# Attention with a convolved query on one core: reordering the start, shortening Newton's step, and fetching the last outputs' operands earlier

## The chip, the cores and the metric

The kernel runs on one core of one Trainium2 chip. The metric is device time in microseconds (us). A profile of one execution shows five engines: TensorE (PE, matrix products; its weight loads are listed apart as PEld), VectorE (DVE), ScalarE (ACT), GpSimd (POOL) and SyncE (SP), which issues most of the DMA transfers. Every engine works through its own instructions in order and waits on semaphores for the others.

## The reference

x has the shape 4 x 384 x 48 x 48: four images of 2304 tokens with 384 channels, in 8 heads of 48.

```python
local = lax.conv_general_dilated(x, conv_w, ...)      # depthwise, 7 x 7, then batch norm
x_norm = _layernorm(x_flat, ln_gamma, ln_beta)        # over the channels
qkv = x_norm @ qkv_w.T + qkv_b
q = q + _layernorm(local_flat, ln_gamma, ln_beta)     # the convolution joins the query
attn = softmax(einsum(q, k) * scale); out = einsum(attn, v)
out = x_flat + out @ proj_w.T + proj_b
```

All is computed in float32.

## The kernel before

**Tiles.** Channels lie on the partitions, in three chunks of 128 (in an order in which every chunk holds the 48 rows of two heads' parts at partitions 0 and 64). Tokens come in groups of 384, that is 8 image rows: 6 groups to an image (`NG`), 24 in all (`NT`). A "product" below is one matmul instruction; the profile lists each float32 product of full size as two PE records.

**Stages.** (1) The start: vectors, taps and weights are loaded and scaled, and group 0 of x is normalized. (2) A loop over the six groups of image 0: `from_x` makes values, keys and queries of group g (three value, three key, three query projections, each of three products), while the next group of x is normalized. (3) For every group t of 24, twelve slots of attention: scores, the exponential on ScalarE (`score`), and the weighted sum (`weigh`). At the beginning of images 1 to 3, `from_x` makes keys and values of that image and the output projection of the image before. (4) The tail: the output projections of the last six groups (18 projections of three products), each followed by `finish`, which adds the residual on VectorE and issues the store.

**The convolution** runs on VectorE, one instruction for a tap and a chunk (`conv_ops`), 147 to a group. For group 0 the first `PE_TAPS` = 10 taps of chunk 0 are done by TensorE instead, with diagonal matrices made on ScalarE (`make_diagonals`, `first_products`) and added by `add_products`. `convolve_first(n)` hands out n conv instructions by hand in the start and in the loop; from then on `plan` spreads them over the slots, from the count that has been done by then.

**A layer norm** (`Norm`) is: the mean over the channels by a product with `mean_w` (`mean_of`, `mean`), `centre`, `squares` on ScalarE, the mean of the squares, `root` on ScalarE (logarithm, exponential, square) and a step of Newton on VectorE (`newton`), then `scale`. For later images `few_root` and `few_newton` do the same on few numbers.

**Scale and shift of the layer norm** are folded into the weights: `scale_values` and `scale_rows` multiply them on ScalarE; `shift_rows` makes the shift's products with the weights as rows, and `columns` turns these into columns for `key_bias` and `query_bias`.

**What sets the order.** TensorE, VectorE and ScalarE have the order in which the code calls them; so have SP and POOL during the first loads. After these a scheduler orders SP's transfers. The transfers of SP and ACT share eight semaphores in turn: a transfer is issued when the one eight places before it has landed. PSUM tiles of two banks come alternately from two pools of two tiles each, `accumulator` (in the profile "o") and `ring` ("r"), through `two_banks`.

**The tail's operands.** The attention outputs of the last five groups but the very last are kept in DRAM (`hold`) and read back (`fetch`, tile "af"); `load_residual` reads x again (tile "xr"). `divide` makes the reciprocal softmax sums of a group and spreads them ("rb"). A count of sums that are out of bounds (`judge`) decides at the end whether a second, slower pass is needed, which isn't with this data.

Of the kernel before, what the change touches and what calls it, by code (L numbers as in the profile page):

```python
# [15 lines left out]
P = 128  # L16
# [13 lines left out]
AHEAD = 8  # L30
# [15 lines left out]
def unshifted_pass(  # L46
# [107 lines left out]
    nc.scalar.dma_start(out=taps_in, in_=conv_w)  # L154
    load_slab(0, 0)
    load_x(0, 0)
# [37 lines left out]
    load_x(0, 1)  # L194
    for g in range(2, NG):
        load_x(0, g)
# [64 lines left out]
    def make_diagonals():  # L261
        for i, tap in enumerate(taps[:PE_TAPS]):
            nc.scalar.mul(diagonal(i), ident, cw[:, 0, tap : tap + 1])
# [86 lines left out]
    class Norm:  # L350
# [52 lines left out]
        def root(self):  # L403

            y, u = self.buf[:, 1, :], self.buf[:, 2, :]
            nc.scalar.activation(u, self.m, AF.Ln, bias=eps)
            nc.scalar.activation(y, u, AF.Exp, scale=-0.5)
            nc.scalar.activation(u, y, AF.Square)

        def newton(self):  # L410
# [3 lines left out]
            nc.vector.scalar_tensor_tensor(u, u, -1.0, y, ALU.add, ALU.mult)  # L414
            nc.vector.scalar_tensor_tensor(y, u, -0.5, y, ALU.mult, ALU.add)
# [38 lines left out]
        def few_root(self):  # L454
# [4 lines left out]
            nc.scalar.activation(self.u, self.y, AF.Square)  # L459

        def few_newton(self):
            u, y = self.u, self.y
            nc.vector.tensor_mul(u, u, self.v)
            nc.vector.scalar_tensor_tensor(u, u, -1.0, y, ALU.add, ALU.mult)
            nc.vector.scalar_tensor_tensor(y, u, -0.5, y, ALU.mult, ALU.add)
# [3 lines left out]
        def scale(self, rs):  # L469
            nc.vector.tensor_mul(self.src, self.src, rs)  # L470
# [83 lines left out]
    row = work.tile([P, CC, P], F32, tag="rb", name="row", bufs=1)  # L554

    def of_row(i):
        return slice(0, 1) if i == 2 else slice(64, 65)

    def shift_rows(some):
        r = two_banks()  # L560
        for c in range(CC):
            for i in some:
# [6 lines left out]
                )  # L569
        for i in some:  # L570
            src, dst = r[of_row(i), i % 2, :C], row[of_row(i)]
            dst = dst.rearrange("o u (h d) -> o u h d", h=2)
            nc.scalar.copy(
                dst[:, :, :, 0:HD], src[:, 0:288].rearrange("o (u h d) -> o u h d", h=2, d=HD)
# [3 lines left out]
                src[:, 288:384].rearrange("o (h u r) -> o u h r", h=2, r=16),  # L578
            )

    def columns(some):

        m = two_banks()[:, :, 0:CC]
        for j, i in enumerate(some):
            for c in range(CC):
                nc.tensor.matmul(
                    m[:, j, c : c + 1],
                    lhsT=row[of_row(i), c, :],
# [18 lines left out]
    def key_bias(m):  # L607
        nc.vector.tensor_add(qkb[:, 1, :], qk_vec[:, 1, :], m[:, 0, :])
        nc.vector.tensor_add(vbp[:, :, 0], vbp[:, :, 0], m[:, 1, :])

    def query_bias(m):

        nc.vector.tensor_add(qkb[:, 0, :], qk_vec[:, 0, :], m[:, 0, :])
# [18 lines left out]
    def local_end(t, rs):  # L632
        acc = accs[t]
        nc.vector.tensor_mul(acc, acc, rs)
# [73 lines left out]
    def load_residual(t):  # L708
        b, g = divmod(t, NG)
        xr = work.tile([P, CC, G], F32, tag="xr", name=f"xr{t}")  # L710
# [11 lines left out]
    def fetch(t):  # L722
        ao = work.tile([P, CC, G], F32, tag="af", name=f"af{t}")
# [92 lines left out]
    make_diagonals()  # L816
    first_products(3)
    norm = Norm(xn[0, 0])
    norm.mean_of(norm.src)
    convolve_first(AHEAD)  # L820
    norm.centre()
    norm.squares()
    first_products(3)
    shift_rows((2, 1))
    scale_values()
    convolve_first(12)
    norm.mean_of(norm.buf)
    norm.root()
    first_products(4)
    m = columns((1, 2))  # L830
    for c in range(CC):
        scale_rows(1, c)
    norm.scale(norm.newton())
    key_bias(m)
    for g in range(NG):
# [4 lines left out]
        convolve_first(4)  # L840
# [5 lines left out]
        convolve_first(5)  # L846
# [3 lines left out]
        if g == 0:  # L850
            shift_rows((0,))
# [4 lines left out]
        if g == 0:  # L856
            for c in range(CC):
                scale_rows(0, c)
        next(making)
        if g == 0:  # L860
            m = columns((0,))
        convolve_first(8 if last else 13)
# [4 lines left out]
        if g == 0:  # L867
            query_bias(m)
# [5 lines left out]
    for t in range(NT):  # L874
# [52 lines left out]
        for s in range(NSLOT):  # L927
# [8 lines left out]
            if s == NSLOT - 4 and g == NG - 1:  # L936
                ao = fetch(t - g)
                if next_image:
                    for gx in range(NG - later(b + 1), NG - 1):
# [623 lines left out]
```

## Time and profile before

| what | us |
|---|---|
| median of 5 runs | 2870.2 (2867.95 to 2871.55) |
| the profiled execution's own time | 2869.94 |
| its span in the profile | 2868.2 |
| first product on TensorE | 11.48 |
| first value projection of group 0 | 29.73 |
| first scores (attention begins) | 151.17 |
| last weighted sum ends, tail begins | 2817.69 |
| last result written by VectorE | 2863.3 |

Starts and durations are in us from the start of the span. A line of the timeline gives start, duration, engine, line of the source and operation, output and inputs, the count, and in brackets how long the engine was idle before it and what released it. The time outside the span, 1.7 us in this execution, is not seen by the profile.

### The profile page before, as it was taken

Reading aid. Unit: us, or ns where it says so; the run is one execution under the profiler, and the core shown is the slowest. Engines: PE = TensorE matmul, PEld = TensorE weight load, DVE = VectorE, ACT = ScalarE, POOL = GpSimd, SP = SyncE. Lnnn points to the kernel's source line nnn. Section 1 sums busy time; section 2 is a strip of 40 time slices with the busy share of each in tenths; the row PEclk is TensorE's granted clock in tenths of the full one; section 3 lists DMA queues with packets and bytes.
Section 4 is the critical chain, followed back from the end, with each engine's and each line's share of the span. In section 5 each row is a group of like instructions: output and inputs, shape, how many; then the busy total and the mean of one; then the engine's idle time right before and its main releaser. Section 6 shows DMA issues by size and latency. Waiting matters only on the chain.

```text
span 2868.2 us, 70244 instructions
## 1 busy us (share of the span) xinstructions
PE 2835.5 (99%) x29492; PEld 1438.0 (50%) x29492; DVE 2353.2 (82%) x4661; ACT 1648.4 (57%) x2341; POOL 17.2 (1%) x82
## 2 busy tenths in 40 slices
PE   8999999999999999999999999999999999999998
PEld 4544454554554455555555445555555544444444
DVE  7999999999888888888888889888788787787302
ACT  4356666666226666666623666666642466666661
POOL 1000000000000000000000000000000000000000
PEclk9999999999999999999999999999999999999999
DMA  6101121101221111110132112102113110100004
GB/s 115 38 7 35 45 49 35 37 25 43 74 80 29 42 35 42 29 39 24 38 94 69 28 30 51 35 22 45 38 39 87 52 22 30 41 23 15 13 21 120
DMA packets 103688, 124.37 MB, mean 43 GB/s; under 512 B 43344, under 2 KB 89024, under 8 KB 103360
## 3 DMA queue, kind: packets, MB, share of 16 engines
q1 hardware_dynamic: 99568, 116.07, 16.8%
q8 instruction: 233, 3.82, 0.6%
q10 hardware_dynamic: 3088, 3.65, 0.4%
q14 instruction: 95, 0.78, 0.1%
q0 software_dynamic: 704, 0.06, 0.0%
HBM read 81.98 MB, written 27.03 MB: 38 GB/s over the span
## 4 chain that ended last, share of the span: by engine, by line
PE 95%; DVE 2%; DMA 2%; ACT 0%; issue 0%; SPq 0%; ACTq 0%; DVEq 0%
PE r L754 39%; PE o L775 39%; PE r L475 9%; PE o L475 8%; DVE acc L255 1%; DMA xn<-in_x_dram 1%; DVE xr L730 0%; DMA out_dram<-xr 0%; DMA rb<-rden 0%; DMA af<-held 0%; DMA taps_in<-in_conv_w_dram 0%; DMA staged<-in_qkv_wT_dram 0%; DMA vec<-natural 0%; DVE xn L401 0%; ACT pt L762 0%
## 5 line engine op out<-in xcount | busy, mean ns | idle before, releaser
L762 ACT ACTIVATE pt<-r 128x768 f32<-128x768 f32 x1728 | 1399.0, 810 | 757.3 <-PE r L754 741.1
L255 DVE SCALAR_TENSOR_TENSOR acc<-slab,vec,acc 128x368 f32<-128x368 f32 (+7 forms) x3447 | 1757.1, 585 | 5.5 <-DMA xn<-in_x_dram 4.4
L775 PE MATMUL o<-pt,v 64*64 64x384 f32 x13824 | 1436.6, 482 | 0.0
L754 PE MATMUL r<-xn,k 48*64 48x384 f32 x10368 | 1080.2, 482 | 3.3 <-DVE xr L730 2.0
L775 PEld LDWEIGHTS o<-pt,v 64*64 64x64 f32 x13824 | 547.7, 132 | 571.0 <-issue 547.5
L754 PEld LDWEIGHTS r<-xn,k 48*64 48x64 f32 x10368 | 412.4, 132 | 432.2 <-issue 374.3
L754 PE MATMUL r<-qt,kt 48*64 48x384 f32 x3456 | 357.7, 482 | 0.1
L754 PEld LDWEIGHTS r<-qt,kt 48*64 48x64 f32 x3456 | 133.4, 132 | 146.5 <-issue 135.9
L673 DVE TENSOR_TENSOR ao<-o,ao 113x384 f32<-113x384 f32 x72 | 40.0, 555 | 194.6 <-PE r L754 177.9
L475 PE MATMUL r<-xn,w_qk 128*128 128x384 f32 x444 | 151.3, 486 | 0.0
L475 PE MATMUL o<-xn,w_qk 128*128 128x384 f32 x420 | 143.1, 486 | 0.0
L475 PEld LDWEIGHTS r<-xn,w_qk 128*128 128x128 f32 x444 | 84.3, 190 | 58.6
L475 PEld LDWEIGHTS o<-xn,w_qk 128*128 128x128 f32 x420 | 79.8, 190 | 55.6
L507 ACT COPY v<-o 128x384 f32<-128x384 f32 x45 | 19.5, 482 | 135.5 <-PE o L475 135.5
L475 PE MATMUL o<-w_v,xn 128*128 128x384 f32 x270 | 93.3, 495 | 2.7 <-DVE xn L470 2.3
L475 PE MATMUL r<-af,w_o 128*128 128x384 f32 x234 | 80.0, 489 | 4.6 <-DVE xr L730 4.3
L673 DVE TENSOR_TENSOR aot<-o,aot 113x384 f32<-113x384 f32 x24 | 13.4, 557 | 77.4 <-ACT aot L664 61.3
L475 PEld LDWEIGHTS o<-w_v,xn 128*128 128x128 f32 x270 | 51.6, 193 | 40.8 <-issue 5.7
L374 DVE TENSOR_TENSOR sq<-sq 128x384 f32<-128x384 f32 x47 | 26.1, 554 | 55.9 <-ACT sq L369 55.9
L475 PEld LDWEIGHTS r<-af,w_o 128*128 128x128 f32 x234 | 44.0, 190 | 37.1 <-DVE xr L730 6.7
L730 DVE SCALAR_TENSOR_TENSOR xr<-o,pb,xr 128x384 f32<-128x384 f32 x25 | 15.4, 618 | 52.3 <-ACT xn L526 42.4
L475 PE MATMUL r<-w_v,xn 128*128 128x384 f32 x162 | 56.2, 486 | 0.0
(130 smaller groups left out, 1027.6 us busy)
## 6 DMA issues: line engine op xcount, KB each, us to landing
xr<-in_x_dram SPq DMA_DIRECT2D x24, 576.0 KB
slab<-in_x_dram SPq DMA_DIRECT2D x32, 378.0 KB
held<-ao SPq DMA_DIRECT2D x20, 576.0 KB
af<-held SPq DMA_DIRECT2D x20, 576.0 KB
xn<-in_x_dram SPq DMA_DIRECT2D x48, 216.0 KB
rb<-rden SPq DMA_DIRECT2D x48, 216.0 KB
out_dram<-xr SPq DMA_DIRECT2D x54, 192.0 KB
slab<-in_x_dram SPq DMA_DIRECT2D x16, 297.0 KB
```

What stands on the lines that cost most here:

```text
L255: nc.vector.scalar_tensor_tensor(dst, src, weight, dst, ALU.mult, ALU.add)
L374: nc.vector.tensor_add(self.buf[:, 0, :], src[:, 0, :], src[:, 1, :])
L475: nc.tensor.matmul(dst, lhsT=weights(c), rhs=src(c), start=c == 0, stop=c == CC - 1)
L507: nc.scalar.copy(v[:, blk, :, 0:HD], r[:, :C].rearrange("p (h d) -> p h d", d=HD))
L673: nc.vector.tensor_add(dst, sums[0 : 64 + HA, 1, :G], dst)
L730: nc.vector.scalar_tensor_tensor(xr[:, co, :], m, pb[:, co : co + 1], xr[:, co, :], ALU.add, ALU.add)
L754: nc.tensor.matmul(r[h, j, :G], lhsT=kk[:, blk * P + h.start : blk * P + h.stop], rhs=qq, start=True, stop=True,)
L762: nc.scalar.activation(pt, r[:, :, :G], AF.Exp, scale=SCALE)
L775: nc.tensor.matmul(sums[halves[j], i, :G], lhsT=values[t // NG, kb // NB][h, first : first + 64], rhs=pt[h, j, :], start=kb == 0, stop=kb ...
```

## The change

Four things are changed.

*The start.* `load_x(0, 0)` is issued ahead of `load_slab(0, 0)`. TensorE begins with twelve products of 128 columns (`WARM`), whose result is overwritten. The mean of x, centring, squares and the mean of the squares come ahead of the conv instructions (now 9 of them) and of the ten tap products, which are spread: 5 after the mean of the squares, 3 after the value row, 2 in the loop. The shift row of the values stays ahead of the loop; those of keys and queries, and all nine columns, go into group 0 of the loop, where 29 conv instructions stand in place of 25 (one is moved from the third to the second place in every group; the last group has 21 for 20). In all, 159 conv instructions are given out before attention, for 165.

*Newton's step.* With u = m y^2 / 2 from ScalarE (the factor is in the square's scale), y (u - 1.5) is the step with its sign turned: two operations for three. `scale` and `local_end` turn the sign back with one operation of two multiplications, in place of one with one.

*The tail's operands.* All six residuals and five fetched outputs are read in the last group, into tiles that are free then ("xn", "acc", "sq", "xr"), in place of one group ahead. In the instruction list that the scheduler makes, each fetch stands right behind its `hold`, in groups 19 to 23.

*The pool parity.* As `two_banks` is called once more ahead of the loop, tiles that were "o" are "r" from there on, and the reverse.

```diff
-AHEAD = 8
+AHEAD = 9
+WARM = 12
...
+    load_x(0, 0)
     load_slab(0, 0)
-    load_x(0, 0)
...
-            nc.scalar.activation(u, y, AF.Square)
+            nc.scalar.activation(u, y, AF.Square, scale=0.5**0.5)
...
             nc.vector.scalar_tensor_tensor(u, self.m, eps, u, ALU.add, ALU.mult)
-            nc.vector.scalar_tensor_tensor(u, u, -1.0, y, ALU.add, ALU.mult)
-            nc.vector.scalar_tensor_tensor(y, u, -0.5, y, ALU.mult, ALU.add)
+            nc.vector.scalar_tensor_tensor(y, u, -1.5, y, ALU.add, ALU.mult)
...
         def scale(self, rs):
-            nc.vector.tensor_mul(self.src, self.src, rs)
+            nc.vector.scalar_tensor_tensor(self.src, self.src, -1.0, rs, ALU.mult, ALU.mult)
...
-    def load_residual(t):
+    def load_residual(t, tag="xr", bufs=2):
...
     def fetch(t):
-        ao = work.tile([P, CC, G], F32, tag="af", name=f"af{t}")
+        if t < NT - NG:
+            ao = work.tile([P, CC, G], F32, tag="af", name=f"af{t}")
+        else:
+            ao = big.tile([P, CC, G], F32, tag=f"xn{t % NG}", name=f"af{t}")
...
-    make_diagonals()
-    first_products(3)
+    for _ in range(WARM):
+        nc.tensor.matmul(first_sum[:, 0:P], lhsT=mean_w, rhs=ident, start=True, stop=True)
     norm = Norm(xn[0, 0])
     norm.mean_of(norm.src)
-    convolve_first(AHEAD)
     norm.centre()
     norm.squares()
-    first_products(3)
-    shift_rows((2, 1))
-    scale_values()
-    convolve_first(12)
+    make_diagonals(0, 5)
+    convolve_first(AHEAD)
     norm.mean_of(norm.buf)
     norm.root()
-    first_products(4)
-    m = columns((1, 2))
+    make_diagonals(5, PE_TAPS)
+    first_products(5)
+    norm.scale(norm.newton())
+    shift_rows((2,))
+    scale_values()
+    first_products(3)
     for c in range(CC):
         scale_rows(1, c)
-    norm.scale(norm.newton())
-    key_bias(m)
     for g in range(NG):
...
         next(making)
-        convolve_first(4)
+        if g == 0:
+            shift_rows((1, 0))
+            rows_out((2, 1, 0))
+            first_products(PE_TAPS - 8)
+        convolve_first(4 if g else 8)
...
             add_products()
-        convolve_first(5)
+            m = columns()
+            key_bias(m)
+            query_bias(m)
+        convolve_first(6)
...
-        if g == 0:
-            m = columns((0,))
-        convolve_first(8 if last else 13)
+        convolve_first(8 if last else 12)
...
             if s == NSLOT - 4 and g == NG - 1:
-                ao = fetch(t - g)
                 if next_image:
+                    ao = fetch(t - g)
...
                 else:
-                    load_residual(t - g)
-                    load_residual(t - g + 1)
-                    coming_ao = fetch(t - g + 1)
+                    places = [("acc", 3)] * 3 + [("sq", 2)] * 2 + [("xr", 2)]
+                    aos = []
+                    for i in range(NG):
+                        load_residual(t - g + i, *places[i])
+                        aos.append(fetch(t - g + i) if i < g else outputs[t][0])
...
     for before in range(NT - NG, NT):
+        ao = aos[before % NG]
...
-        ao = coming_ao
-        if before + 3 < NT:
-            coming_ao = fetch(before + 2)
-        else:
-            coming_ao = outputs[NT - 1][0]
-        if before + 2 < NT:
-            load_residual(before + 2)
```

## The prediction

> **What bounds the kernel now.** I read the busy times by stage first, then the timelines of the start and the tail, then the waits between. By stage (us; busy time and count of each engine, granted clock, DMA share, GB/s):
>
> ```profile
> 36.50:151.00 114.50, 112.43 (x346) 63.86 (x346) 106.83 (x197) 46.40 (x89) 0.00 (x0) 1.00 0.20 42
> 151.00:2816.00 2665.00, 2661.64 (x28951) 1341.72 (x28954) 2209.11 (x4391) 1587.05 (x2216) 2.94 (x36) 1.00 0.16 39
> 2816.00:2868.20 52.20, 39.00 (x134) 20.37 (x126) 13.91 (x26) 1.17 (x2) 0.00 (x0) 0.98 0.55 164
> ```
>
> The first column is TensorE. In attention it lacks 3.4 of 2665 us, so whatever is moved there earlier moves the end. What can be won lies before 151 and after 2816. The timeline of the start:
>
> ```profile
> 11.48 4.16 PE L274 MATMUL o<-slab,pt 128*128 128x384 f32 x6 [11.48 <-ACT pt L263]
> 15.43 2.61 PE L475 MATMUL o<-xn,mean_w 128*128 128x384 f32 x6
> 29.73 5.80 PE L475 MATMUL o<-w_v,xn 128*128 128x384 f32 x12 [2.31 <-DVE xn L470]
> 36.48 2.20 PE L475 MATMUL o<-w_v,xn 128*128 128x384 f32 x6 [0.30 <-ACT v L507]
> ```
>
> The mean of x stands behind three tap products that wait for the taps and diagonals. The value projections begin at 29.73 with a cold array: 12 records in 5.80, where 12 otherwise take 3.87 in the chain of waits. The clock in half-microsecond stages says when it fell and came back (last columns: clock, DMA share, GB/s):
>
> ```profile
> 27.50:28.00 0.50, 0.00 (x0) 1.00 1.03 209
> 30.50:31.00 0.50, 0.50 (x2) 0.50 1.03 209
> 33.50:34.00 0.50, 0.50 (x3) 0.98 1.02 209
> ```
>
> In the loop the chain starts on TensorE, then passes to VectorE:
>
> ```profile
> 67.31 3.87 PE o L475 x12
> 96.77 1.35 DVE xn L401
> 140.61 0.88 PE o L386 x2
> 151.17 0.85 PE r L754 x8
> ```
>
> So both engines nearly set the pace there. Waits of TensorE between 160 and 2800, and then the tail's timeline:
>
> ```profile
> PE r L754 <- DVE xr L730: 2.0, 3, 0.8
> ```
> ```profile
> 2826.33 0.21 PE L1046 MATMUL o<-outside,ones_col 128*1 128x24 f32 x2 [1.66 <-DVE outside L1044]
> 2840.58 2.20 PE L475 MATMUL r<-af,w_o 128*128 128x384 f32 x6 [0.28 <-DMA af<-held]
> 2844.59 2.20 PE L475 MATMUL r<-af,w_o 128*128 128x384 f32 x6 [1.81 <-DVE xr L730]
> 2851.72 2.20 PE L475 MATMUL r<-af,w_o 128*128 128x384 f32 x6 [1.06 <-DVE xr L730]
> ```
>
> The three 0.8 are the beginnings of images 1 to 3. In the tail a second projection waits 0.71 for VectorE in any case; only 1.81 and 1.06 exceed it, for late residuals.
>
> [...] the clock falls near 30.1 and returns near 33.5, after 27.4 to 29.7 without a product. [...] the trace moves 0.40 MB in the first 4 us and 0.74 in the next four.
>
> **The change, step by step** (in us from the start).
>
> *x.* x, taps and vectors are 0.67 MB, so at those rates the bytes are in at 5.5, landed by about 6. The twelve warming products have no row; the nearest is the bias product (128 columns of weights, 18 records in 2.17, 0.12 each, twice that cold), so 24 records end between 4.7 and 7.5. If load and product don't overlap, cold, they end at 12; I take 7.0. Mean: three products 1.94, to 9.0. Centre 1.35, to 10.5; squares 1.16, to 11.8. Before, the squares ended at 20.6.
>
> *Slab and vectors.* By the same rates slab and x are in at about 10.3, landed near 11, where the scaled vectors landed before (ScalarE's first diagonal at 11.02). The 9 conv instructions (8 took 4.89) end at 16.5.
>
> *Normalizing.* Mean of squares 12.0 to 13.9, root (0.58, 0.52, 0.52) to 15.8, but VectorE is at its conv until 16.5; Newton's two (0.62, 0.56) to 17.7, scale 1.36 to 19.1. Meanwhile TensorE has five tap products (3.1), the value row (three, 1.9) and three more taps (1.9): to 20.9. So the value projections start at 20.9 if the array stays warm. It idles 3.0 us from 9.0 to 12.0, [...]. I take 1.5: **22.4**, against 29.73.
>
> *Group 0 of the loop.* From 22.4: values 3.9, two shift rows side by side 2.0 (six took that before), two taps 1.3, mean 0.65, nine columns 1.6 (six took 1.07): 31.8. VectorE has been waiting in `add_products` and then for the columns, about 6 us. Then four tiny additions 0.6, six conv 3.1, centre 1.4, three conv 1.5, sum of squares 1.15: 40.1. TensorE, done with value and key at 35.8, waits 4.4 for it: a stall that stands in place of the removed ones. Mean 0.65, then 9.7 of keys and queries: 50.7. Before, group 1's values began at 54.12. Of 7.3 gained, 3.4 are left (5.5 if warm).
>
> *Groups 1 to 5.* TensorE needs 27 products of 0.645 and two means, 18.75 each, 93.75 in all. Before it took 97.05 (54.12 to 151.17), the 3.3 being waits for VectorE. VectorE now saves one 0.56 operation a group (and the scale costs nothing: 1358 ns for either form, rows L446 and L470), so its groups of 18.8, 17.6, 19.7 and 19.5 busy become 18.2, 17.0, 19.1 and 18.9: level with TensorE, which I take to wait no more than 0.3. Attention begins at 50.7 + 93.75 + 0.3 = 144.8 (142.7 warm): **6.4 won** (8.5).
>
> *Later.* Six conv instructions more (3.4) are left to groups 0 to 2. By the plan's own sums only two of them fall ahead of group 1's mean at 220.4, where the sum was ready 2.3 early, and VectorE ends the loop about 8 earlier: covered. Without the cover each would cost 0.58. Few-number Newton steps save 0.17 each where VectorE idles: nothing.
>
> *Parity.* At the start of images 1 to 3 the last output pair now lies in "o", and the next scores need "r": the 3 waits of 0.76 should go, **2.0 won**. From 0 (another tile is waited for) to 2.3.
>
> *Tail.* Group spans before were 6.81, 6.89, 6.96, 7.98, 7.14, 6.94; at 6.81 each 1.9 goes, and 0.3 for the fetch: **2.1 won**. The 2.0 wait for the count of sums stays: its reciprocal waits for the same small transfers. The fetches: eleven reads of 576 KB, some 3.1 each, now under attention with DMA 0.16 busy. SP waits for `hold` to land ahead of each fetch (2.8 in image 3: 2388.20 to 2391.03), and the next norm's small transfers stand behind; see the last rival.
>
> Sum: 6.4 + 2.0 + 2.1 = 10.5. Against the profiled execution, 2868.2 - 10.5 = 2857.7 of span, plus 1.7 around it, 2859.4; the median is 0.3 higher: **2859.7**.
>
> **Rivals.** *Warm:* the idle 3.0 us doesn't drop the clock; 2.1 more: 2857.6. For it: in the tail, 2.0 idle drops nothing. Against: the fall at 30.1.
>
> *VectorE becomes the bound of the loop:* it idles some 10 us ahead of group 0's centring, and gains at group 1 only 0.5 (its scale ends at 49.1, before 49.58). If TensorE follows it as it did from 96.8 on, what is left at attention is 0.5 and four Newton savings (2.4), about 3: 2863. Against: its groups are then no longer than TensorE's.
>
> *Parity or tail give nothing*, as the hand-over of tiles to VectorE waits in another place: 2861.7 to 2863.8.
>
> *The warming is too long* (ends at 12): x waits, 5 us later, partly hidden by the slab and the taps; some 3 lost: 2862.7.
>
> *Slower:* SP's queue in the last groups. Norm partial sums stand behind hold, fetch and residual reads. Before, group 23's queries were written at 2712.9 and first used at about 2724.5, so 11.6 of delay are free. Behind that SP would have to be late by 11.6 + 10.5 + 5.7 = 28 in one group, or by 17 in three, to end 5.7 slower (2876). Two reads and a landing are 9. It needs a read that waits for a tile that isn't free.
>
> **Chances and range.** Forecast 0.48, of its own 2857 to 2862; warm 0.15; VectorE 0.15; parity or tail 0.12; warming 0.06; slower 0.04. A time within 0.2% (5.7 us; about what a measurement can tell) of 2870.2 is one over 2864.5: it takes two of the losing rivals together. Faster 0.87, same 0.10, slower 0.03. The range reaches from the warm case with the whole parity gain, 2856, to the single losing rivals, 2864.
>
> **What would show it.** Right: first value projection at 21 to 23; then a wait of 4 us for the squares of group 1; attention at 143 to 145; no wait for residuals by L754's successor; the tail's groups at 6.8 each. Wrong: mean of x after 9; VectorE ahead of TensorE's waits up to 140; group 1's mean late; SP behind at the last groups' sums.

## The result and the profile after

| | before | after |
|---|---|---|
| median, us | 2870.11 (44 runs, 2867.11 to 2872.49) | 2866.38 (24 runs, 2864.74 to 2867.87) |
| ratio, 95% interval | | 0.9988 [0.9982, 0.9993] |
| span of the profiled execution | 2868.2 | 2865.4 |
| first value projection | 29.73 | 22.90 |
| group 1's values | 53.95 | 54.84 |
| attention begins | 151.10 | 150.69 |
| first projection of the tail | 2817.62 | 2816.12 |
| last result written by VectorE | 2863.30 | 2859.81 |

The change wins 3.7 us. The forecast was 10.5 (2859.7, range 2856 to 2864), so the prediction is wrong. The table shows where most of it went: the first value projection is 6.8 earlier, and some 30 us later, at group 1's values, nothing of this is left. (Starts in the table are those of TensorE's timeline, before and after. The chain of waits, from which 54.12 and 151.17 were read ahead of the prediction, puts the same starts up to 0.2 later.)

One warning on the profile after: it shows one of the slower executions. Its mean granted clock is 0.997, as in five of the kernel's executions on record, which took 2867.3 to 2867.9; the other 21 have 0.998 and took 2864.7 to 2867.1.

By stage, with the limits moved to where the stages begin (time; busy time and count of TensorE, its weight loads, VectorE, ScalarE, GpSimd; then granted clock, DMA share, GB/s), the profile after:

```profile
36.50:150.50 114.00, 109.39 (x328) 62.67 (x326) 105.19 (x193) 45.66 (x87) 0.00 (x0) 0.97 0.21 43
150.50:2814.50 2664.00, 2661.30 (x28951) 1364.67 (x28954) 2204.52 (x4354) 1586.89 (x2216) 2.94 (x36) 1.00 0.16 41
2814.50:2865.40 50.90, 38.73 (x134) 20.45 (x126) 13.91 (x26) 1.17 (x2) 0.00 (x0) 0.98 0.28 87
```

In the loop TensorE is busy for 109.4 of 114.0, where it was 112.4 of 114.5, and its mean clock is 0.97 in place of 1.00. Attention and tail are as good as or better than before. So the loss is in the loop. TensorE's timeline of the start and of group 0, after:

```profile
7.21 2.17 PE L473 MATMUL o<-xn,mean_w 128*128 128x384 f32 x6 [0.30 <-DMA xn<-in_x_dram]
12.02 3.17 PE L473 MATMUL r<-sq,mean_w 128*128 128x384 f32 x6 [2.64 <-ACT sq L364]
22.90 4.03 PE L473 MATMUL r<-w_v,xn 128*128 128x384 f32 x12
28.28 2.31 PE L563 MATMUL o<-staged,vec 128*1 128x384 f32 x12 [1.35 <-ACT row L578]
32.56 1.49 PE L590 MATMUL o<-one,row 1*128 1x1 f32 x18
41.70 1.62 PE L386 MATMUL o<-sq,mean_w 128*128 128x384 f32 x2 [3.58 <-DVE sq L375]
43.11 6.09 PE L473 MATMUL r<-xn,w_qk 128*128 128x384 f32 x12
54.84 4.03 PE L473 MATMUL o<-w_v,xn 128*128 128x384 f32 x12
```

Three things are to be seen. The rows of key and query wait 1.35 for ScalarE. The mean of the squares of group 1 waits 3.58 for VectorE, which was forecast. And after that wait 12 records take 6.09, where 12 took 4.03 at 22.90, and the mean takes 1.62 in place of 0.81. The clock in stages of half a microsecond says why (it is the third figure from the end):

```profile
40.00:40.50 0.50, 0.00 (x0) 0.00 (x0) 0.50 (x2) 0.50 (x2) 0.00 (x0) 0.92 0.92 177
40.50:41.00 0.50, 0.00 (x0) 0.00 (x0) 0.47 (x2) 0.50 (x3) 0.00 (x0) 0.50 1.06 254
47.00:47.50 0.50, 0.50 (x3) 0.36 (x2) 0.50 (x2) 0.00 (x0) 0.00 (x0) 0.76 0.00 0
```

It fell to half at 40.4, within the wait, and came back at 47.2; from 40.5 to 47.0 it is 0.50. In the chain of waits of the loop (start, duration), VectorE still has a part in four of the five groups after group 0, as before, but a shorter one. Before, the chain stayed on VectorE from 96.77 to 140.48; after, it comes back to TensorE in between:

```profile
97.75 1.35 DVE xn L401
120.99 0.88 PE o L386 x2
136.10 1.35 DVE acc L401
140.20 0.88 PE r L386 x2
150.75 0.85 PE r L761 x8
```

The beginning of image 1, first before and then after:

```profile
858.69 0.88 PE L754 MATMUL r<-xn,k 48*64 48x384 f32 x8
860.33 1.52 PE L754 MATMUL r<-xn,k 48*64 48x384 f32 x16 [0.76 <-DVE xr L730]
861.67 0.83 PE L775 MATMUL o<-pt,v 64*64 64x384 f32 x8
```
```profile
858.33 1.52 PE L761 MATMUL r<-xn,k 48*64 48x384 f32 x16
860.13 0.88 PE L761 MATMUL r<-xn,k 48*64 48x384 f32 x8 [0.28 <-ACT pt L769]
860.83 0.83 PE L782 MATMUL o<-pt,v 64*64 64x384 f32 x8
```

The wait of 0.76 for VectorE's addition is gone. From the first scores to the first weighted sum it was 2.98 and is 2.50: 0.5 of the 0.76 is won, since the third block of scores now waits for an exponential. In the waits of TensorE from 150 to 2805 (total, times, longest) this is all that there is, after:

```profile
PE r L761 <- ACT pt L769: 2.6, 7, 0.8
```

In the tail, after:

```profile
2824.83 0.21 PE L1049 MATMUL r<-outside,ones_col 128*1 128x24 f32 x2 [1.66 <-DVE outside L1047]
2827.88 2.20 PE L473 MATMUL o<-af,w_o 128*128 128x384 f32 x6 [0.71 <-DVE xr L737]
2855.01 2.20 PE L473 MATMUL o<-ao,w_o 128*128 128x384 f32 x6 [0.71 <-DVE xr L737]
```

All groups after the count of sums are alike, with 0.71 before the second projection and none of the longer waits; the wait of 1.66 for the count has stayed.

### The profile page after: what moved, and what is told of

It reads as the page before. It is cut to its first block, busy times and chain, and to the rows that moved or that the text cites. A ratio compares the mean times of both kernels' runs of the same rounds, so it can differ in the third digit from the quotient of the medians.

```text
span 2865.4 us, 70237 instructions
## 1 busy us (share of the span) xinstructions
PE 2839.8 (99%) x29516; PEld 1466.2 (51%) x29516; DVE 2342.3 (82%) x4613; ACT 1648.1 (58%) x2341; POOL 17.3 (1%) x82
## 4 chain that ended last, share of the span: by engine, by line
PE 93%; DVE 6%; ACT 0%; DMA 0%; issue 0%; SPq 0%; DVEq 0%; ACTq 0%
PE r L761 37%; PE o L782 37%; PE r L473 9%; PE o L473 9%; DVE acc L255 5%; PE o L274 0%; ACT pt L769 0%; DVE xn L401 0%; DVE sq L375 0%; DVE xr L737 0%; DVE sq L374 0%; DMA xn<-in_x_dram 0%; PE r L386 0%; PE o L563 0%; PE o L386 0%
## 5 line engine op out<-in xcount | busy, mean ns | idle before, releaser
L782 PEld LDWEIGHTS o<-pt,v 64*64 64x64 f32 x13824 | 559.0, 132 | 559.5 <-issue 517.7
L761 PEld LDWEIGHTS r<-xn,k 48*64 48x64 f32 x10368 | 419.1, 132 | 424.6 <-issue 360.3
L505 ACT COPY v<-r 128x384 f32<-128x384 f32 x45 | 19.5, 481 | 130.2 <-PE r L473 130.2
L473 PE MATMUL r<-w_v,xn 128*128 128x384 f32 x270 | 91.4, 488 | 0.0
L473 PE MATMUL o<-af,w_o 128*128 128x384 f32 x234 | 79.9, 488 | 2.8 <-DVE xr L737 2.8
L473 PEld LDWEIGHTS r<-w_v,xn 128*128 128x128 f32 x270 | 51.0, 190 | 36.4 <-issue 1.8
L473 PEld LDWEIGHTS o<-af,w_o 128*128 128x128 f32 x234 | 44.0, 190 | 35.0 <-DVE xr L737 5.3
L737 DVE SCALAR_TENSOR_TENSOR xr<-r,pb,xr 128x384 f32<-128x384 f32 x25 | 15.4, 618 | 53.9 <-ACT xn L524 44.0
L473 PE MATMUL o<-w_v,xn 128*128 128x384 f32 x162 | 56.2, 486 | 0.0
```

The lines of the kernel that those rows point to most:

```text
L473: nc.tensor.matmul(dst, lhsT=weights(c), rhs=src(c), start=c == 0, stop=c == CC - 1)
L505: nc.scalar.copy(v[:, blk, :, 0:HD], r[:, :C].rearrange("p (h d) -> p h d", d=HD))
L737: nc.vector.scalar_tensor_tensor(xr[:, co, :], m, pb[:, co : co + 1], xr[:, co, :], ALU.add, ALU.add)
L761: nc.tensor.matmul(r[h, j, :G], lhsT=kk[:, blk * P + h.start : blk * P + h.stop], rhs=qq, start=True, stop=True,)
L782: nc.tensor.matmul(sums[halves[j], i, :G], lhsT=values[t // NG, kb // NB][h, first : first + 64], rhs=pt[h, j, :], start=kb == 0, stop=kb ...
```

## The experiments

The kernels were timed in sets, e1 to e4, e5 to e8, e9 to e12 and e13 to e15, each set with the kernel before on the same chip. The third column is the median less that of the kernel before in the same set; the changed kernel stands in it twice.

| run | median | less before | ratio to before, 95% |
|---|---|---|---|
| the changed kernel | 2866.38 | -3.7 | [0.9982, 0.9993] |
| e1_fill | 2864.55 | -4.7 | [0.9978, 0.9991] |
| e2_row | 2864.55 | -4.7 | [0.9976, 0.9990] |
| e3_mean_first | 2860.89 | -8.4 | [0.9961, 0.9982] |
| e4_tail | 2867.58 | -1.7 | [0.9985, 1.0002] |
| e5_parity | 2867.57 | -2.4 | [0.9987, 1.0003] |
| e6_newton | 2866.29 | -3.7 | [0.9980, 0.9993] |
| e7_no_warm | 2869.57 | -0.4 | [0.9990, 1.0006] |
| e8_best | 2861.64 | -8.3 | [0.9964, 0.9982] |
| e9_conv13 | 2864.52 | -4.7 | [0.9978, 0.9991] |
| e10_split | 2863.47 | -5.7 | [0.9973, 0.9988] |
| e11_best13 | 2860.81 | -8.4 | [0.9957, 0.9981] |
| e12_best13_split | 2859.30 | -9.9 | [0.9954, 0.9979] |
| e13_after_again | 2866.54 | -3.1 | [0.9980, 0.9997] |
| e14_fill_split | 2862.39 | -7.2 | [0.9966, 0.9985] |
| e15_fill_split13 | 2862.02 | -7.6 | [0.9964, 0.9983] |

The intervals of the ratios are 3 to 7 us wide, so single steps of 1 us are read from the traces, and from kernels of one set.

### The wait in group 0: clock, rows, or order

**e1: the clock kept up in the wait.** Filler products on x, whose result isn't used, stand ahead of the mean of the squares in group 0.

```diff
-        def mean(self):
+        def mean(self, fill=0):
             self.m = two_banks()[:, 0, :G]
+            for _ in range(fill):
+                nc.tensor.matmul(self.m, lhsT=mean_w, rhs=xn[0, 0][:, 0, :], start=True, stop=True)
...
-        norm.mean()
+        norm.mean(0 if g else 5)
         norm.root()
```

> The changed kernel with five more products of 384 columns (their result is overwritten) on TensorE ahead of the second mean of group 0, where it stood idle from 38.1 to 41.7 and then ran at half clock to 47.7. Theory clock (the idle stretch dropped the clock, and that cost some 3 us): the second mean takes 0.65 and the next 12 records 3.87 in place of 1.62 and 5.88, group 1's values begin at 51.8 in place of 54.84, and attention begins 2 to 3 earlier than 150.69; time 2863.5 to 2864.5. Rival (VectorE sets the pace of the loop, the clock costs nothing): values at 51.8 but attention within 0.5 of 150.69, time as the changed kernel, 2866.4.

TensorE's timeline of this run:

```profile
37.80 3.39 PE L387 MATMUL o<-xn,mean_w 128*128 128x384 f32 x10
41.54 0.88 PE L388 MATMUL o<-sq,mean_w 128*128 128x384 f32 x2 [0.35 <-DVE sq L375]
42.26 4.03 PE L475 MATMUL r<-xn,w_qk 128*128 128x384 f32 x12
```

The mean begins when it did (41.54, in the changed kernel 41.70), and the keys take 4.03. Group 1's values begin at 51.93 in place of 54.84, attention at 147.76 in place of 150.69: 2.9, of which 0.15 is the earlier mean and the rest the clock, in the execution that the trace shows. In the median the filler brings less: 1.0 to 1.6 (4.7 below the kernel before, where the changed kernel was 3.7 and 3.1 below), and the intervals overlap.

**e2: the value row copied out at once.** In the changed kernel the tap sum holds one of the two tiles of "o". The rows of key and query need the other, which is the value row's until ScalarE has copied it, and that copy stood behind the copies of the values.

```diff
     shift_rows((2,))
+    rows_out((2,))
     scale_values()
...
-            rows_out((2, 1, 0))
+            rows_out((1, 0))
```

> The changed kernel with the value row copied out of PSUM on ScalarE right after its products, ahead of the scaling of the weights, so that the key and query rows need not wait for the tile. Theory tile (the rows of keys and queries waited 1.35 for the copy, since the tap sum holds the other tile of the pool): these rows start at 27.0 in place of 28.28, and all of group 0 follows 1.3 earlier; the idle stretch of 3.6 and the half clock stay; attention at 149.4, time 2865. Rival (VectorE's wait for x of group 1 and its own work set the pace): group 1's squares at 41.5 as now, time 2866.4.

The rows begin at 25.79, straight after the values, and the wait of 1.35 is gone. The stall for the squares is 3.78, the clock falls with it again (the keys take 6.22 in place of 4.03), and group 1's values begin at 52.48. That is 2.4 earlier than in the changed kernel, of which 1.15 is an earlier first value projection (21.75) in this execution: the rows' wait was worth about its 1.3.

**e3: group 1's mean ahead of the rows.** Nothing is left out; on TensorE the mean of group 1 stands ahead of the key and query rows and the last taps, on VectorE the six convolution instructions and the centring stand ahead of `add_products` and the bias additions.

```diff
-        if g == 0:
-            shift_rows((1, 0))
-            rows_out((2, 1, 0))
-            first_products(PE_TAPS - 8)
         convolve_first(4 if g else 8)
...
         norm.mean()
         if g == 0:
-            add_products()
-            m = columns()
-            key_bias(m)
-            query_bias(m)
+            shift_rows((1, 0))
+            rows_out((2, 1, 0))
+            first_products(PE_TAPS - 8)
         convolve_first(6)
         norm.centre()
         norm.squares()
+        if g == 0:
+            add_products()
+            m = columns()
+            key_bias(m)
+            query_bias(m)
```

> The changed kernel with group 1's mean ahead of the key and query rows and the last two taps on TensorE, and its six conv instructions and centring ahead of add_products and the biases on VectorE: nothing is left out. Theory order (VectorE waited 6 us in add_products and for the columns with the centring behind it, and this wait became TensorE's idle stretch and half clock): the squares are summed at 37 in place of 41.6, TensorE does not idle there, group 1's values begin at 48 in place of 54.84, attention at 142.5 to 144, time 2858.5 to 2860.5. Rival (the loop is bound by VectorE's amount of work): attention no more than 2 earlier, time 2864.5 or more.

```profile
27.41 0.88 PE L386 MATMUL o<-sq,mean_w 128*128 128x384 f32 x2 [1.71 <-DVE sq L375]
37.09 0.81 PE L386 MATMUL o<-sq,mean_w 128*128 128x384 f32 x2
37.73 4.03 PE L473 MATMUL r<-xn,w_qk 128*128 128x384 f32 x12
47.41 4.03 PE L473 MATMUL o<-w_v,xn 128*128 128x384 f32 x12
```

The stall is gone and the clock stays up behind it: the keys take 4.03. Group 1's values begin at 47.41 and attention at 143.24, 7.4 earlier than in the changed kernel, of which 1.3 is an earlier first value projection (21.59) in this execution. The order takes away three things at once: the stall, the fall behind it and the rows' wait; the wait of 1.71 is new. The median is 8.4 below the kernel before in its set, where the changed kernel was 3.1 to 3.7 below: 4.7 to 5.3 are won by the order of group 0 alone. The rival, a loop bound by VectorE's amount of work, falls.

### The parts alone

**e4: the tail alone**, on the kernel before: the loads of residuals and the fetches in the last group, as in the change.

```diff
...
-                ao = fetch(t - g)
                 if next_image:
+                    ao = fetch(t - g)
...
+                    for i in range(NG):
+                        load_residual(t - g + i, *places[i])
+                        aos.append(fetch(t - g + i) if i < g else outputs[t][0])
...
```

> The kernel before with the change of the tail alone (all residuals and fetched outputs read under the last groups). Theory: the tail from its first projection to VectorE's last result takes 43.6 in place of 45.6, the start is as before; time 2868.1. Rival (the 2 us of the changed kernel's tail come from the other parity of the tiles): 45.6 and 2870.1.

From the tail's first projection (2818.95) to VectorE's last result (2862.64) it takes 43.69; before 45.68, in the changed kernel 43.69. So 2.0 is the tail's own, and it needs nothing of the rest.

**e5: the parity alone**, on the kernel before.

```diff
+    two_banks()
     for g in range(NG):
```

> The kernel before with one tile of TensorE's results asked for and left unused ahead of the loop, so that in attention the last pair of outputs and the next image's first scores lie in other tiles than before; nothing is left out. Prediction's step on parity: the three waits of 0.76 for VectorE's residual addition at the starts of images 1 to 3 go and 2.0 us are won from the start of attention to the start of the tail (2666.5 before). Rival, from the trace of the changed kernel: the first scores find their tile free but the second pair of scores then waits for ScalarE's exponentials, so half of it comes back: 0.9 to 1.3 won. Second rival: nothing. In time, against before: -2.0, -1.0 or 0.

From attention (149.80) to the tail (2814.94) it takes 2665.14, before 2666.52: 1.4 won. Where the starts of the exponentials are compared one by one with those of the kernel before, the trace gains 0.47, 0.51 and 0.15 at the starts of the three images, 1.1 in all. At image 1 the picture is the changed kernel's (0.28 for ScalarE in place of 0.76 for VectorE). The first rival is right: part of the gain comes back as a wait for an exponential.

**e6: Newton's step alone**, on the kernel before, in both norms and with the sign in the scaling.

```diff
-            nc.scalar.activation(u, y, AF.Square)
+            nc.scalar.activation(u, y, AF.Square, scale=0.5**0.5)
...
-            nc.vector.scalar_tensor_tensor(u, u, -1.0, y, ALU.add, ALU.mult)
-            nc.vector.scalar_tensor_tensor(y, u, -0.5, y, ALU.mult, ALU.add)
+            nc.vector.scalar_tensor_tensor(y, u, -1.5, y, ALU.add, ALU.mult)
...
```

> The kernel before with Newton's step in two operations alone (start, order, parity and tail as before); nothing is left out. Prediction's step on groups 1 to 5: waits of TensorE for VectorE fall from 3.3 to 0.3, so the stretch from group 1's values to attention (97.05 before) falls to about 94.1, and the time by 3. Rival, from the changed kernel and three variants, which all have 95.8 there: TensorE's second mean in a group still finds the sum of squares not there by some 0.2 [...], whatever the Newton step costs; then 95.8 to 96.4, and the time falls by 0.6 to 1.2. Second rival: nothing at all, 97.0.

The loop from group 1's values (52.75) to attention (149.27) takes 96.52, so 0.6 of 97.15 is won, not 3; the rival's size. What was not foreseen lies after it: 2664.05 from attention to the tail, 2.5 less than before. By the exponentials 1.7 of it comes at 180 and 0.7 to 0.8 in three steps, at 405, 499 and 592. These steps are put down to Newton's shorter step on few numbers, as nothing else was changed there. The 1.7 is no effect of the edit. The kernel before has there:

```profile
177.65 2.17 PE L475 MATMUL r<-vbp,w_o 128*128 128x1 f32 x18
179.75 1.07 PE L754 MATMUL r<-xn,k 48*64 48x384 f32 x8
180.58 1.52 PE L775 MATMUL o<-pt,v 64*64 64x384 f32 x8
```

Here the products that make the output's bias, of one column each, are followed by scores and sums that take 1.52 in place of 0.83: the clock has fallen, and is 0.50 from 180.5 to 183.5. In e6 it is 1.00 from 170 to 188, and the same stretch is followed by 0.83. By the scores and sums behind it, the clock fell here in the profiles of before, after, e1, e2, e4, e5, e8 and e13, and not in e3, e6, e7, e9 and e11. Such a fall belongs to the kernel before as much as to the changed one.

**e7: the warming products taken away** from the changed kernel.

```diff
-WARM = 12
+WARM = 0
```

> The changed kernel without its twelve warming products; nothing is left out. If they keep the clock up as the change says: the mean of x starts at about 6 (not 7.2) but at half the clock, takes about 4 in place of 2, and the value projections start 0.5 to 2 us later than 22.9; time +0.5 to +2. Rival, the warming is too long: x has landed before it ends, and without it the mean ends earlier than 9.4 and the values start up to 1.2 earlier, time -1. Second rival: VectorE's convolution, which starts when the scaled vectors land at 14.0 and stands ahead of Newton's step, sets the start of the values, so that neither moves them by more than 0.3.

```profile
6.97 4.06 PE L473 MATMUL o<-xn,mean_w 128*128 128x384 f32 x6 [6.97 <-DMA xn<-in_x_dram]
24.55 4.03 PE L473 MATMUL r<-w_v,xn 128*128 128x384 f32 x12
```

x has landed at 6.97, so the warming, which ends at 6.9, delays nothing, and without it the mean takes 4.06 in place of 2.17 (at a granted clock of 1.00 in the changed kernel) and the values begin 1.65 later. The warming does what it is for; the median is 3 worse, with an interval of about 3 on that.

### Six convolution instructions

In e7's trace something else was to be seen. After the wait of 3.57 for the squares of group 1 its clock hadn't fallen (1.00 in every stage from 27 to 49), nor at the bias products (0.83 for the sums behind them), and it lost 2.4 in a wait in attention. The scores behind that wait take 1.56, where they take 0.88 in the changed kernel: there the clock did fall.

```profile
311.22 1.56 PE L761 MATMUL r<-xn,k 48*64 48x384 f32 x8 [2.40 <-ACT pt L769]
```

The changed kernel, with VectorE's, ScalarE's and TensorE's timelines there:

```profile
309.74 1.36 DVE L445 SCALAR_TENSOR_TENSOR acc<-sq,acc 128x1152 f32<-128x1152 f32 x1
```
```profile
311.14 0.52 ACT L369 ACTIVATE sq<-acc 128x384 f32<-128x384 f32 x1 [1.82 <-DVE acc L445]
311.57 0.79 ACT L769 ACTIVATE pt<-r 128x768 f32<-128x768 f32 x1
```
```profile
312.41 0.88 PE L761 MATMUL r<-xn,k 48*64 48x384 f32 x8 [0.79 <-ACT pt L769]
```

VectorE's centring for group 2 ends late, ScalarE's squares wait for it, the exponentials stand behind the squares, and the scores need a tile that an exponential frees. In the trace the exponential at 311.57 starts right behind the squares of 311.14 and 3.06 after the one ahead of it (308.51), where 1.29 is usual. Before, ScalarE's squares waited 0.88 there and TensorE didn't.

**e9: the six instructions that the change leaves to attention, made in the loop.** The change takes eleven out of the start and puts five more into the loop, so that six are left over. The lines give the loop six more:

```diff
-        convolve_first(8 if last else 12)
+        convolve_first(9 if last else 13)
```

> The changed kernel with the six convolution instructions that it leaves to attention made in the loop again (13 in place of 12 in groups 0 to 4, 9 in place of 8 in the last); nothing is left out. Theory: these six are not covered in attention, they make VectorE late for the centring at the end of group 0 (it ends 160.4 after the start of attention, 157.8 where they had been made), ScalarE's exponentials stand behind the squares that wait for it, and TensorE waits 0.8 at 312 (2.4 where the clock hadn't dropped at 180). Then the wait at 312 goes, the stretch from attention to the tail falls from 2665.4 to 2664.3 or less, and the loop gives up less than that: -0.5 to -2 against the changed kernel. Rival, the prediction's: the six are covered in attention, and in the loop they cost what they cost TensorE before, 0.2 to 1 in waits for VectorE: attention later by that, no gain after it, time +0.2 to +1. Second rival: the wait at 312 comes from something else and stays.

ScalarE's wait there, in this run:

```profile
306.67 0.52 ACT L369 ACTIVATE sq<-acc 128x384 f32<-128x384 f32 x1 [0.86 <-DVE acc L445]
```

That is 157.8 after the start of attention (148.86), in the changed kernel 160.45, and TensorE has no wait. The loop takes 96.96 (changed kernel 95.85), attention to the tail 2662.96 (2665.43; 2665.76 in e7, where the clock didn't fall at the bias products either). So the six cost 1.1 in the loop, and against e7 2.8 in attention, some 1.3 of which is the fall of the clock at 311 in e7. They are not covered, as the theory had it. The pair e14 and e15 below has none of these falls, and there they cost 1.5 in attention against 1.1 in the loop: what is won by moving them is the small difference of the two.

### The two places where the clock falls

**e10: the bias products in three parts**, in three slots, in the changed kernel.

```diff
...
-    def output_bias():
...
+    def output_bias(co):
...
-            if t == 0 and s == CC:
-                output_bias()
+            if t == 0 and CC <= s < 2 * CC:
+                output_bias(s - CC)
```

> The changed kernel with the products of one column that make the output's bias (18 records in 2.17 us at 177) in three parts, in three slots in place of one; nothing is left out. Theory: such a stretch lets the clock fall, [...] and costs 1.7 in those executions (five of eight profiles have it); in parts it never falls. But VectorE is late at 312 in this kernel, and there TensorE gives back 1.6 of the 1.7 (its wait of 0.8 becomes 2.4): time within 0.6 of the changed kernel's. Rival: the 1.7 is kept, and the median falls by about 1.0. Second rival: the clock falls all the same, at another place.

The clock doesn't fall there (the sums behind each part take 0.83), and attention to the tail takes 2664.19, 1.2 less than in the changed kernel (the wait at 308 is 0.79, not 2.4). That is the rival's number, but the clock isn't the whole reason, as the split changes a second thing. In the changed kernel VectorE waits for the bias at this place, and in parts it doesn't; the changed kernel, then e10:

```profile
179.62 0.16 DVE L631 TENSOR_TENSOR pb<-pb,added 128x3 f32<-128x3 f32 x1 [1.27 <-ACT added L630]
```
```profile
175.32 0.16 DVE L631 TENSOR_TENSOR pb<-pb,added 128x1 f32<-128x1 f32 x1
```

So VectorE ends its centring for group 2 159.2 after the start of attention, in the changed kernel 160.4. In e7 only the fall is missing, and VectorE waits as in the changed kernel. There the wait at 311 takes back 1.6 of the 1.7, and with the fall in that wait the stretch to the tail is no shorter than the changed kernel's (2665.76 against 2665.43). VectorE does take the gain back, unless its own wait goes too.

The same run, with the changed kernel's code up to there, shows that the wait in group 0 doesn't always drop the clock:

```profile
41.50 0.89 PE L386 MATMUL o<-sq,mean_w 128*128 128x384 f32 x2 [3.57 <-DVE sq L375]
42.22 4.03 PE L473 MATMUL r<-xn,w_qk 128*128 128x384 f32 x12
```

The wait is the same, the clock is 1.00 from 36.5 to 42.5, and the keys take 4.03. Group 1's values begin at 51.90.

To see how much of the median this is, the last set had three more: **e13**, the changed kernel itself; **e14**, with the filler of e1 and the split of e10 together; **e15**, e14 with e9's edit.

> The changed kernel as it is, beside the next two. Theory: its executions differ by which of two places (the wait of group 0, 2.9; the bias products, 1.2 to 1.7) [...], so they lie 3 to 4 us apart and the median is 3 to 4 below the kernel before; in the profile both, one or neither is seen. Rival: the spread is that of any kernel, 1 to 2, and the profile shows both falls again.

> The changed kernel with five filler products in the wait of group 0 and the bias products in three parts: the clock falls in neither place; nothing is left out. Theory: the median is 2 to 4 below the changed kernel's in the same call, the executions lie within 2 us. Rival: the clock fell in few executions only, and the median moves by less than 1; then the missing gain lies with VectorE.

> The kernel before this one in the list with the six convolution instructions in the loop again; nothing is left out. Theory: VectorE is no longer late at the end of group 0 of attention and in the groups after it: loop 1.1 longer, the stretch after it 2.5 to 2.8 shorter, median 1 to 1.7 lower. Rival: once the clock no longer falls at the bias products, the plan's cover is as good as the loop's: within 0.5.

The changed kernel gave 2866.54 with executions 3.96 apart; its profile has the fall in group 0 in part (keys 5.34) and at the bias products. With the filler and the split the median is 2862.39, 4.15 lower, and the executions are 1.6 apart. So the two edits together bring 4.15, by the clock and, with the split, by VectorE's wait for the bias too. Sets timed apart give 1.0 to 1.6 for the filler alone (e1) and 2.0 to 2.6 for the split alone (e10). The spread goes with the clock in single executions: in e9 the five with a mean clock of 0.997 took 2866.4 to 2866.9, the two with 1.0 took 2862.5.

With the six in the loop the median is 2862.02, which is within 0.5: the rival. In the traces 1.5 is won in attention and 1.1 lost in the loop.

### A better order

**e8** is e3 with the value row copied at once and the last two tap products ahead of group 1's mean; **e11** is e8 with the six convolution instructions in the loop; **e12** is e11 with the bias in three parts. Of e8's edit, what it has beyond e2 and e3:

```diff
         norm.sum()
+        if g == 0:
+            first_products(PE_TAPS - 8)
         norm.mean()
         if g == 0:
             shift_rows((1, 0))
             rows_out((1, 0))
-            first_products(PE_TAPS - 8)
```

> The changed kernel with group 1's mean ahead of the key and query rows (as in the run that had 2860.9), the value row copied out as soon as it is made, and the last two tap products ahead of group 1's mean; nothing is left out. In the run with the mean first, TensorE waited 1.7 at 25.7 for the sum of group 1's x, with the two tap products of 1.5 standing behind; ahead of it they fill that wait. Theory that the start is TensorE's work in order and its waits: attention begins 1.0 to 1.5 before 143.2, and the time is 2859.4 to 2860. Rival: VectorE sets group 1's second mean from here on, attention moves by less than 0.4, and the time is 2860.5 to 2861.

> The kernel with group 1's mean first, the value row copied at once and the last two taps ahead of that mean (2861.6), with the six convolution instructions in the loop again; nothing is left out. Theory as for the changed kernel with them: attention no more than 1 later, the stretch after it 1 to 2.5 shorter, time 2859.5 to 2861. Rival: VectorE has less idle time in this order's group 0 (it idles 2.3 us in all between 23 and 48) and the six move the first means of the groups: attention 2 or more later, time 2861.6 to 2863.

> The kernel before this one in the list with the output bias in three parts as well; nothing is left out. Theory: with VectorE no longer late at the end of group 0, what the clock doesn't lose at 170 to 180 is kept: 1 below that kernel, and its executions lie closer together (spread of 2 to 3 in place of 3.5). Rival: no difference, the wait for VectorE at the end of group 0 takes it back.

e8: the rival is right. The taps fill the 1.7, but then the columns wait 1.27 for VectorE's centring; attention begins at 142.87, 0.4 before e3's. e11: attention begins at 147.04, 4.2 later than in e8, so the rival's part on the loop is right. 1.1 of it is the loop, 1.2 the first mean, and most of the rest the clock, which in this execution fell in the rows and columns of group 0, with a values projection of 3.88 in place of 2.20 (3.77 in e12):

```profile
32.69 1.47 PE L590 MATMUL o<-one,row 1*128 1x1 f32 x18 [1.39 <-DVE xn L401]
34.09 3.88 PE L473 MATMUL r<-w_v,xn 128*128 128x384 f32 x6
```

The stretch from attention to the tail is 2.6 shorter than e8's, but e8's profile has the fall at the bias products and e11's hasn't, so that some 1.7 of the 2.6 may be this fall. The medians are equal against the kernel before. e12 is the fastest of all, 2859.30, 1.5 below e11 in the same set, but the intervals overlap, so that 1.5 isn't settled. e3, e8, e11 and e12 all beat both kernels, by 8 to 10 against the one before.

## Why the prediction was wrong

By its own steps, from the profiled executions of before and after (forecast, then measured):

| step | forecast | measured |
|---|---|---|
| first value projection | 22.4 | 22.90 |
| group 1's values | 50.7 | 54.84 |
| groups 1 to 5 | 94.05 | 95.85 |
| won at the start of attention | 6.4 | 0.4 |
| won from there to the tail | 2.0 | 1.1 |
| won in the tail | 2.1 | 2.0 |
| the end's landing | 0 | 0.7 lost |
| won in the span | 10.5 | 2.8 |

**x, normalizing, first values: right.** x landed near 7 (forecast 6), the clock did fall behind the first idle stretch (0.50 from 13.25 to 16.25; the mean of the squares took 3.17, and 2.20 in e8, where it didn't fall), and the values began within 0.5 of the forecast. The terms within are off: VectorE's convolution began at 14.03, not 11.0, as it waited until then for the scaled vectors to land, and that put Newton's step at 19.42, not 16.5. TensorE's work in between hid nearly all of it.

**Group 0 of the loop: the step that failed.** It foresaw the stall for group 1's squares (4.4; measured 3.58) and priced it as time without products only. It left out what the stall does next: in the profiled execution the clock fell in it, and the mean, keys and the rest took 2.7 more than where it didn't fall (13.1 from the mean to group 1's values; 10.4 in e1 and e10). The prediction had allowed 1.5, its author's estimate, for a fall of the clock after the idle time at 9 to 12, and nothing for the longer one that it had itself put at 35.8 to 40.1. The second thing left out is the tile: with the tap sum holding one of two, the rows wait 1.35 for the value row's copy (e2). And a sum slipped: the step's own terms put the squares at 39.6 and group 1's values at 49.9, not at 40.1 and 50.7.

The profiled execution has the fall at nearly its full cost. In other profiles with the same stall it cost 2.9 (e2), 1.7 (e13) or nothing (e7, e9, e10), and in the median the filler brought 1.0 to 1.6. What the median shows clearly is the whole of this step: another order in group 0 (e3) brings 4.7 to 5.3, of the 6.8 by which the gain fell short. The fall at the bias products is no part of that shortfall, since the kernel before has it too.

**Groups 1 to 5: sized wrong.** The forecast took TensorE's waits from 3.3 to 0.3. Measured, the second mean of a group still finds the sum of squares up to 0.4 late, and after such a wait its two records take 0.88 of the chain, not 0.66. A group takes 0.4 more than its products: 95.85, the same within 0.02 in e1, e2, e3 and e7, though attention began up to 7 us apart. The forecast called VectorE level with TensorE, but its own figures had VectorE longer in two of four groups (19.1 and 18.9 against 18.75). Of the 1.3 won, Newton's step alone has 0.6 (e6); where the rest comes from isn't shown.

**"Later" and the few Newton steps: not nothing, in both directions.** Six convolution instructions were costed at nothing, with VectorE's time at the end of the loop as cover. The cover isn't there at the centring for group 2: 0.8 in the profile after, 2.4 where the clock hasn't fallen at the bias products (e7), none with the six in the loop (e9). To make them in the loop costs 1.1, nearly as much, so the sum is hardly moved (e15 against e14: 0.4). Newton's step on few numbers won some 0.7 (e6), where nothing was forecast. These two and the parity give the 1.1 of the table: 1.4 and 0.7 won, 0.9 lost.

**Parity: right in kind, too large in size.** 1.1 to 1.4 in place of 2.0 (e5). The blocks of scores wait for exponentials as soon as they don't wait for VectorE.

**Tail: right**, 2.0 for 2.1, alone (e4) and in the change. The span shows 0.7 less of it, as the last store took 5.6 to its end in place of 4.9 in this execution; e4's took 4.4, so that this is no effect of the edit.

**Rivals.** "VectorE becomes the bound of the loop" gave 2863 for a gain of 3 at attention. No rival but "slower" reached 2866, and the mechanism of this one isn't what happened: with the fillers (e1) the loop after group 0 takes the same 95.83, and all that group 0 gains stays. "Slower" by SP's queue didn't come.

With the fall in group 0 taken out (e1) the span is 5.8 shorter than before, and 4.7 of the 10.5 are still missing: 1.2 at group 1's values, 1.8 in groups 1 to 5, 0.8 from attention to the tail, 0.1 in the tail and 0.7 at the end.

## What to carry to other kernels

A stall that is moved isn't priced by its length: ask whether the array's clock may fall in it, and count the slow products behind it, for every stall that the forecast itself creates. Here a stall of 3.57 to 3.78 dropped the clock in three of six profiles, at 1.7 to 2.9 each. Where VectorE is nearly full, work taken out of one stage lands in another, and the price there is found at the next instruction for which ScalarE's queue waits (here 0.8 of TensorE's time at 312, 2.4 in e7). Where executions of one kernel differ by 4 us, a single trace against a single trace can mislead by as much as the effect sought; take the falls of the clock out (a filler, or parts in place of one run of small products; in e14 they left the executions 1.6 apart, in e13 they are 3.96 apart) before comparing. And ask what else such an edit changes: the parts also took a wait of 1.27 from VectorE.

## What the runs showed of the hardware

Away from a fall or a return the granted clock reads 1.00 or 0.50 in these traces. Half clock lasted 3.4 in the kernel before (30.1 to 33.5, and 180.3 to 183.7), and in the changed one 3.4 (13.1 to 16.5, and 180.4 to 183.8) and twice that (40.4 to 47.2). At the falls of 30.1, 13.1 and 40.4 TensorE had last stopped for want of work 2.3 to 3.7 earlier: at 27.4, 9.4 and 38.1.

The same stall of 3.57 to 3.78 dropped the clock in the profiles of after, e2 and e13, where 12 records of the keys behind it take 6.09, 6.22 and 5.34, and not in e7, e9 and e10, where they take 4.03. What decides between the two isn't shown.

The bias products of one column, 18 records in 2.17 without a pause, were followed by a fall in eight of 13 profiles, though TensorE's records fill that time; in the kernel before the clock is still 1.00 while they run, and falls at 180.3. Six records at a time, 0.83 each (e10, e12, e14, e15), were followed by none. Why it fell in eight and not in the other five isn't shown.
